# A hybrid layer of scan, attention and experts: gate, convolution and the end of attention in another order within a step

## The chip, the cores and the metric

The kernel runs on one core of a Trainium2 chip. Its engines each work through their own instructions: TensorE (PE, matmuls), VectorE (DVE), ScalarE (ACT), GpSimd (POOL) and SyncE (SP, which here only issues DMAs). The metric is the device time of one execution in microseconds; lower is better. Three executions of the kernel before took 10,580.3, 10,592.63 and 10,608.76 us: the median is 10,592.63.

## The reference, cut to what matters

The input x is 16 images of 128 channels by 64x64 pixels, so 16 sequences of T=4096 tokens with 128 channels. Layer 0 is a state-space layer on the group-normed input, with 256 inner channels and 16 states:

```python
xz = u @ W_in;  xs, z = split(xz)            # 128 -> 256 + 256
xc = silu(conv(xs, conv_w, 4 taps, causal) + conv_b)
dt, Bm, Cm = split(xc @ W_xproj)             # 8 + 16 + 16
delta = softplus(dt @ W_dt + b_dt);  A = -exp(A_log)
h_new = exp(delta * A) * h + (delta * xc) * B      # a scan over the 4096 tokens, for each state
y = sum over states of h * C  + xc * D
x = x + (y * silu(z)) @ W_out
```

Layer 1 is an attention with running softmax (8 heads, each with one fixed query, cumulative over the tokens) on layer-normed tokens, and then experts:

```python
k, v = silu(ln(t) @ W_kv)                    # 8 heads x 128 each
s = q . k;   m_A = cummax(s);   e = exp(s - m_A);   u_A = cumsum(e)
t = t + mean over heads of cumsum(e * v) / u_A
t = t + experts(ln(t))                       # each of 64 experts takes its best 8 tokens
```

All arithmetic is float32, apart from some bf16 pieces inside the kernel.

## The kernel before, in words

**Blocks and steps.** The work of layer 0 and of the attention is cut into NK = 128 blocks of L = 512 tokens, 8 blocks per image. One loop over k (L713) runs both, interleaved. In its step k the scan works on block k (`cur`); block k-1 (`prev`) has its y turned back, gated and projected out; block k+1 (`nxt`) is normed, convolved and projected to delta, B and C; and the attention works on block k-9 (`m`: keys, scores, weights, values), on k-10 (`mp_`: the second half of its tokens) and on k-8 (`mn`: layernorm). Steps 0 to 8 have no attention; the last ten have no scan. After the loop come the routing, the experts and the last sum, which the change does not touch.

**States.** Within a step, a loop over the 16 states n (L896) does for each: the product `bx` of delta·x and B (DVE, L355); then `beside(n)` (L737), a list of pieces of all the other work, written out by hand for each n; then decays (ACT exps, L679), the load of B and C for a later state (SP, tile `bct`, L344), the two scans of the state (DVE, L361) with `between(n)` (L725) between them, the product with C (POOL), a copy of the last column (POOL), for some states a DMA that adds two products, and the sums over states on PE into `y_ps` (L388).

**What sets the order.** Every instruction goes through a small class `InOrder` (L23), which keeps the program's order on its engine; for that reason all of them carry line L31 in the profile. No scheduler moves anything. An engine that waits holds up all that follows it in this order. So `beside` and `between` are the schedule.

**Buffers.** [...] One bank is for the scores and the attention's sums (`s_ps`, `ao_ps`), two are for y, two for `bx`. The other three are a pool (`ps`, L83, given out by `bank`, L224) that goes round in the order of requests: keys, values, `yb_ps` (y turned back), `w_ps` (log weights), `o_ps` (output projection), `xs_ps` (convolution), `rest_ps`, `dbl_ps`, `z_ps`, `dt_ps` and others. A request that gets a bank waits until the last reader of its earlier content is done.

**The pieces that the change moves.** `turn_y` (L410) transposes y into two banks at n=2, and `gate` (L417) multiplies each by silu(z) on DVE. `out_proj` (L427) does four matmuls with W_out and two with the identity, which add the residual. `conv(k, a, taps)` (L286) is a convolution half `a` of the 256 channels: two matmuls for each tap with its shifted input. `conv_silu` (L295) does both silus on ACT. `weights(m, c)` (L607) forms the log weights of the 128 tokens c by matmuls and takes their exps on ACT into `wm`; `attend` (L624) multiplies them with the values and forms the carried sums, `carry_on` (L645) copies these out, and `attend_before` (L649) adds what came before the 128 tokens. `add_x` (L655) adds the residual and `finish` (L660) scales the result on ACT and writes it out with a DMA that ACT issues. `score_max` (L521) and `score_less` (on DVE) take the running maximum of the scores, `score_exp` the exp (ACT), `score_sum` the running sum (DVE) and `score_log` (L554) its log (ACT). `rest`, `split` (L568, L577) cut the logs into three bf16 parts, which `store_parts` (L581) writes out as `pd` and `spread_parts` (L586) reads back in 16 small DMAs into the tiles `lh` and `rh`, the inputs of `weights`. `store_bc` (L318) writes B and C out as `bcs`, from where `load_bc` reads them back, copied to all partitions. `gn_end` (L242) finishes, in five parts, the group norm of the next image, in one step of eight.

Of the kernel before, what the change touches and what calls it, by code (L numbers as in the profile page):

```python
# [11 lines left out]
ALU = mybir.AluOpType  # L12
# [27 lines left out]
def conv_attn_hybrid(ctx: ExitStack, tc: tile.TileContext, x, w_in, conv_w, conv_b, w_xproj, w_dt, b_dt,  # L40
# [8 lines left out]
    NH2 = DI // P  # L49
# [31 lines left out]
    with ExitStack() as st:  # L81
# [136 lines left out]
        def load_exp():  # L218
            tc.keep_in_program_order(nc.scalar.preload_act_table_set(EXP_LN))  # L219
# [194 lines left out]
                for c in range(L // P):  # L414
                    PE.transpose(yb[:, bass.ts(c, P)], w["yt"][:, c, bass.ts(a, P)], ident)

        def gate(k):  # L417
            w = blocks[k]
            for a in range(NH2):
                DVE.tensor_tensor(w["z"][:, a, :], w[f"yb{a}"], w["z"][:, a, :], ALU.mult)  # L420

        def tokens_of(w):

# [3 lines left out]
        def out_proj(k):  # L427

            w = blocks[k]
            w["o"] = bank("o_ps")  # L430
            for a in range(NH2):
                PE.matmul(w["o"], wo[:, a, :], w["z"][:, a, :], start=(a == 0), stop=False)
            PE.matmul(w["o"].rearrange("p (j i) -> p j i", j=L // HH), ident, tokens_of(w), start=False, stop=True)
# [211 lines left out]
        def carry_on(m, c):  # L645

            ACT.copy(carry[:, c, :], att[m].pop(("cp", c))[:, :P])

        def attend_before(m, c):  # L649
            s = att[m]  # L650
            if m % NBLK or c:
                PE.matmul(s["o"][:, bass.ts(c % 2, P)], carry[:, (c - 1) % 4, :], s["e"][:, c, :], start=False,
                          stop=True, skip_group_check=True)
# [59 lines left out]
        for k in range(NK + LAG + 1):  # L713
            b, i = divmod(k, NBLK)
            cur = k if k < NK else None
            prev = k - 1 if 0 <= k - 1 < NK else None
# [20 lines left out]
            def beside(n):  # L737

                if n == 0:
                    if mp_ is not None:  # L740
                        attend_before(mp_, 1)
                        add_x(mp_, 0)
                    if m is not None:
                        key(m, 0), key(m, 1), key(m, 2)
                    if mp_ is not None:
                        finish(mp_, 0)
                    if prev is not None:
                        if N - 3 in PAIRS:
                            add_y(prev, N - 3)
                        else:  # L750
                            add_y(prev, N - 2)
                if n == 1:
                    if m is not None:
                        key(m, 3), key(m, 4)
                        score(m, 0)
                    if prev is not None:
                        if N - 3 in PAIRS:
                            add_y(prev, N - 2)
                        add_y(prev, N - 1)
                    if nxt is not None:  # L760
                        norm_block(nxt)
                    if cur is not None:
                        skip(cur)
                    if prev is not None:
                        take_y(prev)
                if n == 2:
                    if m is not None:
                        key(m, 5), key(m, 6), key(m, 7)
                    if prev is not None:
                        turn_y(prev)  # L770
                    if cur is not None:
                        add_y(cur, -1)
                if n == 3:
                    if m is not None:
                        score(m, 1)
                    if prev is not None:
                        gate(prev)
                    if mp_ is not None:
                        for x in range(4, 8):
                            value(mp_, x // 2, x % 2)  # L780
                if n == 4:
                    load_exp()
                    if m is not None:
                        score_max(m)
                    if mp_ is not None:
                        weights(mp_, 2)
                    if ends is not None:
                        gn_end(ends, 1)
                if n == 5:
                    if mp_ is not None:  # L790
                        attend(mp_, 2)
                        weights(mp_, 3)
                    if m is not None:
                        score_exp(m)
                    if prev is not None:
                        out_proj(prev)
                    decays(k, n, 2)
                    if mp_ is not None:
                        carry_on(mp_, 2)
                if n == 6:  # L800
                    if mp_ is not None:
                        attend(mp_, 3)
                        attend_before(mp_, 2)
                    if nxt is not None:
                        conv(nxt, 0)
                    decays(k, n, 2)
                    if prev is not None:
                        put_back(prev)
                    if mp_ is not None:
                        carry_on(mp_, 3)  # L810
                    if ends is not None:
                        gn_end(ends, 3)
                if n == 7:
                    if mp_ is not None:
                        attend_before(mp_, 3)
                        add_x(mp_, 1)
                    if m is not None:
                        score_log(m)
                    if mp_ is not None:
                        finish(mp_, 1)  # L820
                    if m is not None:
                        rest(m, 1)
                        split(m, 1)
                    if nxt is not None:
                        conv(nxt, 1, range(KC // 2))
                    decays(k, n, 2)
                    if m is not None:
                        rest(m, 2)
                        split(m, 2)
                        store_parts(m)  # L830
                        inverse(m)
                    if nxt is not None:
                        conv(nxt, 1, range(KC // 2, KC))
                    if nxt is not None:
                        conv_silu(nxt)
                    if ends is not None:
                        gn_end(ends, 4)
                if n == 8:
                    if cur is not None:
                        sums_of_y(n)  # L840
                    if m is not None:
                        turn_weights(m)
                        value(m, 0, 0)
                    if nxt is not None:
                        xproj(nxt)
                        store_bc(nxt)
                    if m is not None:
                        value(m, 0, 1)
                if n == 9:
                    if mn is not None:  # L850
                        ln_center(mn)
                        ln_square(mn)
                    if cur is not None:
                        gate_silu(cur)
                    if k + 2 < NK:
                        load_block(k + 2, ACT)
                    if m is not None:
                        value(m, 1, 0), value(m, 1, 1)
                if n == 10:
                    if mn is not None:  # L860
                        ln_var(mn)
                    if nxt is not None:
                        delta(nxt)
                    load_exp()
                    if mn is not None:
                        ln_scale(mn)
                if n == 12:
                    if m is not None:
                        weights(m, 0)
                if n == 13:  # L870
                    if m is not None:
                        attend(m, 0)
                        attend_before(m, 0)
                        weights(m, 1)
                    decays(k, n, 2)
                    if m is not None:
                        carry_on(m, 0)
                if n == 14:
                    if mn is not None:
                        ln_apply(mn)  # L880
                    if m is not None:
                        attend(m, 1)
                    decays(k, n, 2)
                    if m is not None:
                        carry_on(m, 1)
                if n == 15:
                    if stat is not None:
                        gn_stats(*stat)
# [7 lines left out]
            for n in range(N):  # L896
# [2 lines left out]
                if ends is not None and n == 2:  # L899
                    gn_end(ends, 0)  # L900
                beside(n)
                if n in (4, 11, 12, 15):
                    decays(k, n, 2)
                if cur is not None:
                    later = k * N + n + LEAD_BC
# [320 lines left out]
```

## Time and profile before

| | |
|---|---|
| median of three executions | 10,592.63 us (10,580.3 to 10,608.76) |
| the profiled execution | 10,585.55 us |
| its span (first to last instruction) | 10,583.8 us |
| PE, DVE busy | 9294.7 us (88%), 9048.4 us (85%) |
| ACT, POOL busy | 7298.5 us (69%), 7402.2 us (70%) |
| mean granted clock of TensorE | 0.933 |
| loop over k with scan and attention | about 640 to 9255 us |
| HBM | 143 GB/s over the span |

Times in the profile are in us from the span's start. In its lists of instructions, `out<-in` are the program's tile names, a number after x is a count, and a bracket tells how long the engine was idle just before and which instruction's end released it. PEld is the loading of weights, which runs beside the matmuls. The ends of matmuls are modelled, so a busy PE isn't always a PE at its peak rate.

### The profile page before, as it was taken

Reading aid. Unit: us, or ns where it says so; the run is one execution under the profiler, and the core shown is the slowest. Engines: PE = TensorE matmul, PEld = TensorE weight load, DVE = VectorE, ACT = ScalarE, POOL = GpSimd, SP = SyncE. Lnnn points to the kernel's source line nnn. Section 1 sums busy time; section 2 is a strip of 40 time slices with the busy share of each in tenths; the row PEclk is TensorE's granted clock in tenths of the full one; section 3 lists DMA queues with packets and bytes.
Section 4 is the critical chain, followed back from the end, with each engine's and each line's share of the span. In section 5 each row is a group of like instructions: output and inputs, shape, how many; then the busy total and the mean of one; then the engine's idle time right before and its main releaser. Section 6 shows DMA issues by size and latency. Waiting matters only on the chain.

```text
span 10583.8 us, 163130 instructions
## 1 busy us (share of the span) xinstructions
PE 9294.7 (88%) x58461; PEld 5670.1 (54%) x58461; DVE 9048.4 (85%) x9987; ACT 7298.5 (69%) x12924; POOL 7402.2 (70%) x4387
## 2 busy tenths in 40 slices
PE   5679999999999999999999999999999999988775
PEld 3345555555555555555555555555555555555652
DVE  8999999999999999999999999999999999921743
ACT  4567777777777777777777777777777777755740
POOL 7888787778787777878777878877787878810000
PEclk7789999999999999999999999999999999999886
DMA  6676666666666666666666766666666666611348
GB/s 172 172 188 171 179 169 180 165 179 173 162 183 161 183 166 181 173 177 170 170 177 168 185 166 186 170 178 170 176 167 173 178 165 181 161 50 39 110 157 355
DMA packets 889083, 1794.66 MB, mean 170 GB/s; under 512 B 96896, under 2 KB 182544, under 8 KB 881104
## 3 DMA queue, kind: packets, MB, share of 16 engines
q1 hardware_dynamic: 732912, 1414.88, 46.4%
q0 software_dynamic: 73728, 268.47, 12.8%
q10 hardware_dynamic: 81632, 100.88, 3.0%
q8 instruction: 463, 7.59, 0.3%
q14 instruction: 348, 2.85, 0.1%
HBM read 1363.98 MB, written 151.52 MB: 143 GB/s over the span
## 4 chain that ended last, share of the span: by engine, by line
PE 61%; ACT 25%; DVE 5%; issue 4%; DMA 3%; POOL 1%; ACTq 1%; SPq 0%; DVEq 0%; POOLq 0%
PE ao_ps L31 9%; PE v_ps L31 9%; PE k_ps L31 8%; ACT da L31 8%; PE y_ps L31 6%; PE carry_ps L31 4%; PE o_ps L31 4%; PE xs_ps L31 4%; ACT wm L31 3%; ACT L219 3%; PE s_ps L31 3%; PE dbl_ps L31 3%; PE dt_ps L31 2%; DVE h L31 2%; PE z_ps L31 2%
## 5 line engine op out<-in xcount | busy, mean ns | idle before, releaser
L31 POOL TENSOR_TENSOR da<-h,bct 128x1024 f32<-128x1024 f32 x2048 | 6600.5, 3223 | 1815.7 <-DVE h L31 812.8
L31 DVE TENSOR_TENSOR_SCAN h<-da,state,bx 128x512 f32<-128x512 f32 x3584 | 4415.2, 1266 | 169.7 <-DVE bx L31 1.9
L31 DVE TENSOR_TENSOR bx<-du,bct 128x1024 f32<-128x1024 f32 x2048 | 2653.7, 1296 | 160.4 <-DMA bct<-bcs 92.0
L31 ACT ACTIVATE da<-delta,a_neg 128x512 f32<-128x512 f32 x4096 | 2628.0, 716 | 42.6 <-DMA da<-da 42.4
L31 PE MATMUL y_ps<-ident,da 128*128 128x128 f32 x12288 | 1800.4, 302 | 237.5 <-DMA da<-da 129.6
L31 PEld LDWEIGHTS y_ps<-ident,da 128*128 128x128 f32 x12288 | 1575.8, 157 | 659.4 <-issue 375.1
L31 PE MATMUL v_ps<-wv,xn 128*128 128x512 f32 x2048 | 1053.8, 639 | 306.8 <-ACT xc L31 299.0
L31 PE MATMUL ao_ps<-wm,v 128*128 128x128 f32 x8192 | 1055.1, 283 | 180.5 <-ACT wm L31 180.5
L31 PEld LDWEIGHTS ao_ps<-wm,v 128*128 128x128 f32 x8192 | 994.1, 195 | 401.6 <-ACT wm L31 246.3
L31 ACT ACTIVATE v<-v_ps 128x512 f32<-128x512 f32 x1024 | 610.2, 597 | 758.3 <-PE v_ps L31 718.0
L31 PE MATMUL k_ps<-xn,wk 128*128 128x512 f32 x2048 | 942.6, 593 | 0.0
L31 PE MATMUL xs_ps<-xb,wc 128*128 128x512 f32 x2048 | 938.0, 594 | 1.8 <-issue 1.8
L31 PEld LDWEIGHTS v_ps<-wv,xn 128*128 128x128 f32 x2048 | 349.9, 195 | 832.7 <-ACT xc L31 326.7
L31 ACT ACTIVATE wm<-w_ps 128x512 f32<-128x512 f32 x1024 | 552.1, 591 | 340.2 <-PE w_ps L31 338.3
L31 ACT ACTIVATE kt<-k_ps 128x512 f32<-128x512 f32 x1024 | 599.5, 600 | 234.4 <-PE k_ps L31 211.5
L31 DVE TENSOR_TENSOR_SCAN h<-da,bx 128x512 f32<-128x512 f32 x512 | 599.9, 1206 | 25.5 <-ACT da L31 0.5
L31 PEld LDWEIGHTS xs_ps<-xb,wc 128*128 128x128 f32 x2048 | 361.6, 191 | 380.5 <-issue 366.0
L31 PEld LDWEIGHTS k_ps<-xn,wk 128*128 128x128 f32 x2048 | 370.2, 190 | 318.5 <-issue 282.9
L31 POOL COPY state<-h 128x2 f32<-128x2 f32 x1792 | 518.1, 289 | 0.0
L31 POOL DMA_DIRECT2D da<-da x512 | 449.1, 877 | 92.1 <-POOL state L31 35.7
L31 ACT ACT_TABLE_LOAD x395 | 506.8, 1283 | 7.7 <-issue 1.5
L31 ACT ACTIVATE xs<-ao_ps 128x256 f32<-128x256 f32 x256 | 97.5, 381 | 438.3 <-PE ao_ps L31 438.3
(196 smaller groups left out, 10679.1 us busy)
## 6 DMA issues: line engine op xcount, KB each, us to landing
bct<-bcs SPq DMA_DIRECT2D x2048, 512.0 KB
da<-da POOLq DMA_DIRECT2D x512, 512.0 KB, 7.9
xs<-t_d SPq DMA_DIRECT2D x240, 256.0 KB
xs<-in_x_dram SPq DMA_DIRECT2D x128, 256.0 KB
xt<-in_x_dram SPq DMA_DIRECT2D x64, 512.0 KB
t_d<-xt SPq DMA_DIRECT2D x64, 512.0 KB
t_d<-xs ACTq DMA_DIRECT2D x256, 128.0 KB
t<-t_d SPq DMA_DIRECT2D x128, 256.0 KB
```

Of the source, the lines that this page charges most:

```text
L31: return lambda *args, **kw: self.tc.keep_in_program_order(f(*args, **kw))
L219: tc.keep_in_program_order(nc.scalar.preload_act_table_set(EXP_LN))
```

## The change

Pieces of `beside` are moved; nothing is added to the computation or taken from it. `gate` now does one half per call.

- The gate of block k-1, both halves at n=3 before, is done half by half: half 0 at n=4 ahead of the running maximum, half 1 at n=5.
- The first half of the convolution of block k+1 moves from n=6 (behind the attentions 2 and 3) to n=4, behind the log weights 2 and ahead of attention 2.
- The log weights 3 and the output projection move from n=5 to n=6.
- The last three pieces of the attention of block k-10 (`attend_before` 3, `add_x`, `finish`) move from n=7, where they were ahead of `rest`, `split` and the second half of the convolution, to n=8, behind the convolution's silus; `attend_before` 2 moves from n=6 to the end of n=5.
- Log weights 0, attention 0 and its carry move one state earlier (n=12, 13 to n=11, 12), with the decays of n=12 behind the attention; log weights 1 stay at n=13.
- The last part of the group norm moves from the end of n=7 to the end of n=8.

```diff
-        def gate(k):
-            w = blocks[k]
-            for a in range(NH2):
-                DVE.tensor_tensor(w["z"][:, a, :], w[f"yb{a}"], w["z"][:, a, :], ALU.mult)
+        def gate(k, a):
+            w = blocks[k]
+            DVE.tensor_tensor(w["z"][:, a, :], w[f"yb{a}"], w["z"][:, a, :], ALU.mult)
...
                 if n == 3:
                     if m is not None:
                         score(m, 1)
-                    if prev is not None:
-                        gate(prev)
                     if mp_ is not None:
                         for x in range(4, 8):
                             value(mp_, x // 2, x % 2)
                 if n == 4:
                     load_exp()
+                    if prev is not None:
+                        gate(prev, 0)
                     if m is not None:
                         score_max(m)
                     if mp_ is not None:
                         weights(mp_, 2)
+                    if nxt is not None:
+                        conv(nxt, 0)
                     if ends is not None:
                         gn_end(ends, 1)
                 if n == 5:
+                    if prev is not None:
+                        gate(prev, 1)
                     if mp_ is not None:
                         attend(mp_, 2)
-                        weights(mp_, 3)
                     if m is not None:
                         score_exp(m)
-                    if prev is not None:
-                        out_proj(prev)
                     decays(k, n, 2)
                     if mp_ is not None:
                         carry_on(mp_, 2)
+                        attend_before(mp_, 2)
                 if n == 6:
                     if mp_ is not None:
+                        weights(mp_, 3)
+                    if prev is not None:
+                        out_proj(prev)
+                    if mp_ is not None:
                         attend(mp_, 3)
-                        attend_before(mp_, 2)
-                    if nxt is not None:
-                        conv(nxt, 0)
                     decays(k, n, 2)
...
                 if n == 7:
-                    if mp_ is not None:
-                        attend_before(mp_, 3)
-                        add_x(mp_, 1)
                     if m is not None:
                         score_log(m)
-                    if mp_ is not None:
-                        finish(mp_, 1)
-                    if m is not None:
                         rest(m, 1)
                         split(m, 1)
...
                         conv_silu(nxt)
-                    if ends is not None:
-                        gn_end(ends, 4)
                 if n == 8:
                     if cur is not None:
                         sums_of_y(n)
+                    if mp_ is not None:
+                        attend_before(mp_, 3)
+                        add_x(mp_, 1)
+                        finish(mp_, 1)
                     if m is not None:
                         turn_weights(m)
                         value(m, 0, 0)
...
                     if m is not None:
                         value(m, 0, 1)
+                    if ends is not None:
+                        gn_end(ends, 4)
...
+                if n == 11:
+                    if m is not None:
+                        weights(m, 0)
                 if n == 12:
-                    if m is not None:
-                        weights(m, 0)
-                if n == 13:
                     if m is not None:
                         attend(m, 0)
                         attend_before(m, 0)
+                    decays(k, n, 2)
+                    if m is not None:
+                        carry_on(m, 0)
+                if n == 13:
+                    if m is not None:
                         weights(m, 1)
                     decays(k, n, 2)
-                    if m is not None:
-                        carry_on(m, 0)
...
-                if n in (4, 11, 12, 15):
+                if n in (4, 11, 15):
                     decays(k, n, 2)
```

## The prediction

> **What bounds the kernel now.** I read the page first: busy shares, the 40 slices, and the chain of work that ended last.
>
> ```profile
> PE 9294.7 (88%) x58461; PEld 5670.1 (54%) x58461; DVE 9048.4 (85%) x9987; ACT 7298.5 (69%) x12924; POOL 7402.2 (70%) x4387
> PEclk7789999999999999999999999999999999999886
> PE 61%; ACT 25%; DVE 5%; issue 4%; DMA 3%; POOL 1%; ACTq 1%; SPq 0%; DVEq 0%; POOLq 0%
> ```
>
> PE and DVE are about equally busy, but the chain is PE and ACT. The steady part runs from 640 to 9255 us: some 118 steps of k at a mean of 73.0 us. Steps 0 to 8 (about 65 us each) lack the attention, those from k=128 (about 48 us) lack the convolution. So the change is worth what it does to one steady step, times 118.
>
> Next, the waits between 2000 and 8000 us, which is 82 steps (columns: total us, times, longest).
>
> ```profile
> PE v_ps L31 <- ACT xc L31: 209.4, 82, 2.6
> DVE z L31 <- PE yb_ps L31: 148.7, 82, 2.8
> PE ao_ps L31 <- ACT wm L31: 101.9, 163, 1.9
> PE o_ps L31 <- ACT wm L31: 60.7, 82, 0.7
> ACT v L31 <- DMA bct<-bcs: 28.0, 8, 4.6
> ```
>
> Per step PE loses 2.55 us waiting for the convolution's silus, 1.24 before the attentions and 0.74 before the output projection; with smaller ones, 5.9 of 73. The gate makes DVE wait 1.8 us per step, but the chain inside a step goes from PE to ACT and back and never through the gate. Third, the timeline of PE, DVE and ACT in one step without disturbance. I count its times from the end of the second score matmul, 4954.98; the step is 71.85 us long.
>
> ```profile
> 4952.69 1.29 DVE L31 TENSOR_TENSOR z<-yb_ps,z 128x512 f32<-128x512 f32 x2 [1.08 <-PE yb_ps L31]
> 4957.52 0.41 DVE L31 TENSOR_TENSOR_SCAN mx<-negc,s_ps 128x128 f32<-128x128 f32 x1
> 4961.20 2.09 PE L31 MATMUL ao_ps<-wm,v 128*128 128x128 f32 x16 [0.91 <-ACT wm L31]
> 4972.23 3.60 PE L31 MATMUL xs_ps<-xb,wc 128*128 128x512 f32 x8
> 4977.40 0.39 ACT L31 ACTIVATE xs<-ao_ps 128x256 f32<-128x256 f32 x1 [4.19 <-PE ao_ps L31]
> 4984.98 1.13 PE L31 MATMUL v_ps<-wv,xn 128*128 128x512 f32 x2 [2.55 <-ACT xc L31]
> 4986.04 1.91 PE L31 MATMUL dbl_ps<-xc,wx 128*40 128x512 f32 x4
> 4988.60 0.33 ACTq L31 DMA_DIRECT2D bcs<-dbl  x1
> ```
>
> The same x-projection one step later, in PE's timeline:
>
> ```profile
> 5058.02 3.21 PE L31 MATMUL dbl_ps<-xc,wx 128*40 128x512 f32 x4
> ```
>
> And both stretches in the windows view (length; busy us of PE, PEld, DVE, ACT, POOL; granted clock; DMA share; GB/s):
>
> ```profile
> 5055.00:5062.00 7.00, 5.04 (x7) 1.31 (x8) 6.70 (x6) 3.88 (x7) 6.44 (x3) 0.76 0.74 203
> 4983.00:4990.00 7.00, 5.02 (x11) 1.74 (x12) 6.70 (x6) 4.60 (x9) 6.41 (x3) 1.00 0.67 184
> ```
>
> After the 2.55 us wait the clock drops to half in about every second step, and four x-projection matmuls take 3.21 us instead of 1.91. Together with the values beside them such a step loses 1.65 us; over the steps, about 0.7.
>
> [...] stretches at 0.5 start on a grid of 3.41 us. [...] In the timeline no matmul overtakes another, so one that waits for a bank holds up all later ones. [...]
>
> **The change part by part**, per steady step.
>
> *Gate in two states.* Same two DVE instructions, 0.65 us each. At n=3 they waited 1.8 us; at n=4 and 5 PE has long turned y, so the wait goes. It was slack: 0 on the chain by itself. But gate 0 (0.65) and gate 1 now stand in other places. Score's maximum starts at 2.5 before and about 3.1 after; from there to the next product DVE takes 4.30 us (4957.52 to 4961.82), then product 5 1.14 and gate 1 0.69: gate 1 ends 6.13 us after the maximum starts. Meanwhile both turned halves hold their banks longer. In the built program the four values of n=3 get the remaining bank and that of gate 0, so weights 2 must wait for a silu of the last value: its end goes from 4.2 to 4.95. The first convolution half gets the bank of gate 1: **a new wait of PE for DVE**. Its matmuls could start at 5; gate 1 ends at 6.35 at the earliest. Cost 1.2 to 1.6 us. Queued behind it: y sums, attention 2, carry, weights 3, o, so everything.
>
> *Convolution half ahead of attention 2.* Eight matmuls, 3.44 us, moved. They cover the 0.91 us wait for wm (ACT ready at 6.2). Gain 0.91. The 0.74 before o remains, since o follows weights 3 by the same 1.47 us and takes over a bank that ACT's exps read.
>
> *End of attention behind the silus.* Two matmul groups (0.22 of earlier state, 0.43 of x) go from before rest to after the y sums, into the 2.55 us wait: PE's work is the same, the wait shrinks by 0.65 to 1.9. On ACT one scaling (0.39) and one DMA issue (0.33) move behind two splits, the issue of pd and the silus. ACT waited 4.19 us for that scaling; now it waits for rest instead, which is on time either way (0). The moved DMA to t_d is read only after the steady phase (0). But SP's and ACT's DMAs are dealt round over eight completion semaphores, each waiting for the previous DMA on its own. By program order bcs now follows the first of the 16 spread transfers lh<-pd, which is issued about 6.9 us after pd and lands some 1.4 later: 8.3, where ACT reaches bcs at 7.3. **ACT stalls about 1.0 us in every step**; queued behind are the value's silu, the square and the gate's silus, and PE waits for them through their banks. About 0.4 of it reaches PE. In return the old neighbour goes: in one step of eight bcs waited 4.6 us for a bct (the last line of the waits above), which cost PE 3.11 and the step about 2.9, or 0.36 on average.
>
> *Weights, attention, carry of m one state earlier, decays behind.* No instruction added. They cover waits of PE for wm (0.43 at 48.8) and carry (0.37). PE gains about 0.45 there at most; but then the key matmuls merely come earlier, and the loop below does not pass through them. 0.
>
> *gn_end 4* moves one state later, in one step of eight, off nothing: 0.
>
> **The sum.** PE alone: 0.75 (weights 2) + 1.35 (gate 1) − 0.91 − 0.65 + 0.4 (bcs) − 0.45 gives +0.5; but the first two waits make up for each other when DVE comes early. I prefer the loop that binds. DVE, from rstd to gate 1: xn and product 0 8.83, four states of 3.85 (15.4), product 4 1.14, gate 0 0.61, maximum stretch 4.30, product 5 1.14, gate 1 0.69: 32.1. PE and ACT from there back to rstd: convolution 3.44, y 0.87, attention 2 with carry and earlier state 3.24, weights 3 to o 1.47, o 3.52, attention 3 2.79, y 0.87, then rest to the value 7.8, value to rstd 15.8, bcs 0.4: 40.2. Together 72.3 for a clean step, 72.6 if bcs costs more than 0.4; I take 72.45 against 71.85: +0.6. Against that, the drops of the clock (0.7) become rare, since the idle time is 1.9 and not 2.55 with real matmuls ahead; I keep 0.25 of it, bounded by 0 and 0.9. And 0.36 of the eighth step goes. So 72.45 + 0.25 = 72.7 against 73.0: −0.3 × 118 = −35 us. The step before: 71.85 + 0.7 + 0.36 is 72.9, the measured 73.0 nearly. Head and tail steps: at most 0.5 us of 9 each, neglected.
>
> The profiled execution took 10,585.55 us (span 10,583.8), 7 below the median of 10,592.63. The change is applied to the median: **10,557 us**.
>
> **Rivals.** *Faster by 1 to 2%.* DVE doesn't bind: it reaches gate 1 before PE wants the bank, because without the wait at the gate (1.8) it runs ahead. For: DVE is 93% busy in the steady part, hence 5 us of slack in a step. Against: xn already waits for rstd in 45 of 82 steps, which ties DVE's start to PE. PE alone then gives 71.85 − 0.91 − 0.65 + 0.75 = 71.05, with 0.25 left of the cold clock: −1.7 × 118, some 10,390 to 10,420.
>
> *Slower.* Convolution behind gate 1: each us by which gate 1 is later than 6.35 holds PE's queue in full. The change breaks even where the clean step reaches 72.75 with 0.25 of cold clock, so where the wait is 0.3 us longer than in my loop. With 1 us more (or the new idle of PE at the convolution dropping the clock, 1.65 in half of the steps), the step is 73.7: +80 us, some 10,675.
>
> *No change.* The removed waits were slack of DVE and ACT (the chain, with 5% of DVE, speaks for it), and the PE waits removed come back at gate 1: 10,590.
>
> **How the numbers follow.** The loop above 0.5 (its own range 10,500 to 10,600, from 0 to 0.9 of cold clock and 0.3 either way on the loop), faster rival 0.2, slower 0.2, no change 0.1. A tenth is left out on either side, half of each outer rival: 10,420 to 10,665. A run of this kernel can tell about 0.3%, 32 us. Of the loop's 0.5, 0.28 lies beyond that, 0.16 within, 0.06 slower. Faster 0.48, same 0.26, slower 0.26.
>
> **What would show it.** Right: no wait of DVE for yb; a wait of xs_ps for DVE z of about 1.3 us in every step; v for xc at 1.9; no ACT wait of 4.19; ACT 1 us behind bcs for lh; fewer x-projections of 3.2 us. Wrong: a wait at xs_ps near 0 (the faster rival) or above 2.5 (the slower), a step time below 71.5 or above 73.3, or the clock lost at a new place.

## The result, and the profile after

The changed kernel took 10,510.32 us (median of three, 10,500.43 to 10,519.05), against 10,592.63 before: a ratio of 0.993, 95% interval 0.9914 to 0.9946, or 82 us. That is inside the stated range and on the side that was forecast, but the gain is more than twice the 36 us of the forecast.

The page of the kernel after: busy shares, granted clock by slices, chain of the work that ended last.

```profile
PE 9306.2 (89%) x58461; PEld 5584.4 (53%) x58461; DVE 8947.7 (85%) x9987; ACT 7317.3 (70%) x12924; POOL 7411.9 (71%) x4387
...
PEclk7789999999999999999999999999999999998886
...
PE 46%; DVE 23%; ACT 18%; issue 9%; DMA 4%; ACTq 1%; SPq 0%; POOL 0%; DVEq 0%; POOLq 0%
```

Busy times hardly differ. The chain does: DVE has gone from 5% to 23% of it. The waits between 2000 and 8000 us, now 83 steps (total us, times, longest), say where it enters:

```profile
PE v_ps L31 <- ACT xc L31: 137.5, 83, 1.7
...
DVE xn L31 <- ACT rstd L31: 107.1, 81, 3.0
...
PE xs_ps L31 <- DVE z L31: 98.8, 83, 1.4
...
PE o_ps L31 <- ACT wm L31: 62.0, 83, 1.0
...
ACT v L31 <- DMA lh<-pd: 8.1, 5, 2.1
...
PE ao_ps L31 <- ACT wm L31: 5.2, 10, 0.6
```

DVE no longer waits for yb. PE's wait for the silus is 1.66 us a step (2.55 before), the one ahead of the attentions is nearly gone (5.2 us in all against 101.9), and a new one stands in every step: the convolution for gate 1, 1.19 us. One clean step in the timelines of DVE, PE, SP and ACT (scores done at 4977.42):

```profile
4977.35 0.68 DVE L31 TENSOR_TENSOR z<-yb_ps,z 128x512 f32<-128x512 f32 x1
...
4983.06 0.68 DVE L31 TENSOR_TENSOR z<-yb_ps,z 128x512 f32<-128x512 f32 x1
...
4983.80 3.70 PE L31 MATMUL xs_ps<-xb,wc 128*128 128x512 f32 x8 [1.25 <-DVE z L31]
...
5007.74 1.12 PE L31 MATMUL v_ps<-wv,xn 128*128 128x512 f32 x2 [1.66 <-ACT xc L31]
5008.80 1.91 PE L31 MATMUL dbl_ps<-xc,wx 128*40 128x512 f32 x4
...
5008.89 0.26 SPq L31 DMA_DIRECT2D lh<-pd  x1
...
5011.35 0.33 ACTq L31 DMA_DIRECT2D bcs<-dbl  x1
```

The x-projection takes 1.91 us here, and in all 118 steps it takes under 2.3; before, 56 of 118 took 2.4 to 3.6. The rest of this document counts in such steps, from the end of one second score matmul to the next. A matmul is called cold here when it runs at half clock. In the traces of both kernels the granted clock is 1.00 or 0.50, nothing between: the windows view of the kernel before has 0.50 from 5058.48 to 5061.88, which takes in most of the prediction's x-projection of 3.21 us. Before, all 243 stretches at 0.50 start on multiples of 3.41 us, counted from the first, to within 0.02 us.

| 118 steps | before | after |
|---|---|---|
| mean, us | 73.00 | 72.31 |
| a clean step (the most frequent length without group norm and without a cold matmul), us | 71.85 | 71.5 |
| PE time lost to half clock, about, us per step (busy time above the median of all steps: x-projection, values, convolution, output projection, delta) | 0.97 | 0.56 |
| mean of the 14 steps with the group norm, us | 75.2 | 75.0 |

The sum of the steps fell by 81.0 us of the 85.1 us between the two spans. So half of the gain is the clean step (−0.35), and the other half is of the size of what the clock takes less (−0.4; a cold matmul can also fall into a wait, so the two need not add up to the 0.69 exactly).

### The profile page after: what moved, and what is told of

Same layout as the page of the kernel before. It is cut to its first block, busy times and chain, and to the rows that moved or that the text cites. A ratio compares the mean times of both kernels' runs of the same rounds, so it can differ in the third digit from the quotient of the medians.

```text
span 10498.7 us, 163128 instructions
## 1 busy us (share of the span) xinstructions
PE 9306.2 (89%) x58461; PEld 5584.4 (53%) x58461; DVE 8947.7 (85%) x9987; ACT 7317.3 (70%) x12924; POOL 7411.9 (71%) x4387
## 4 chain that ended last, share of the span: by engine, by line
PE 46%; DVE 23%; ACT 18%; issue 9%; DMA 4%; ACTq 1%; SPq 0%; POOL 0%; DVEq 0%; POOLq 0%
DVE h L31 11%; DVE bx L31 8%; ACT da L31 7%; PE ao_ps L31 6%; PE y_ps L31 6%; PE v_ps L31 5%; PE xs_ps L31 4%; PE o_ps L31 4%; PE carry_ps L31 3%; PE k_ps L31 3%; PE dt_ps L31 2%; PE dbl_ps L31 2%; PE z_ps L31 2%; PE w_ps L31 2%; ACT wm L31 2%
## 5 line engine op out<-in xcount | busy, mean ns | idle before, releaser
L31 DVE TENSOR_TENSOR bx<-du,bct 128x1024 f32<-128x1024 f32 x2048 | 2608.0, 1273 | 261.9 <-DMA bct<-bcs 195.0
L31 ACT ACTIVATE da<-delta,a_neg 128x512 f32<-128x512 f32 x4096 | 2603.0, 718 | 35.7 <-DMA da<-da 30.6
L31 PE MATMUL y_ps<-ident,da 128*128 128x128 f32 x12288 | 1773.8, 297 | 203.5 <-POOL da L31 103.8
L31 PEld LDWEIGHTS y_ps<-ident,da 128*128 128x128 f32 x12288 | 1534.0, 153 | 629.2 <-issue 372.6
L31 PE MATMUL v_ps<-wv,xn 128*128 128x512 f32 x2048 | 1031.5, 625 | 207.2 <-ACT xc L31 193.8
L31 PE MATMUL xs_ps<-xb,wc 128*128 128x512 f32 x2048 | 987.9, 620 | 141.3 <-DVE z L31 139.5
L31 PE MATMUL ao_ps<-wm,v 128*128 128x128 f32 x8192 | 1027.8, 279 | 54.7 <-ACT wm L31 45.3
L31 PEld LDWEIGHTS v_ps<-wv,xn 128*128 128x128 f32 x2048 | 317.0, 188 | 758.6 <-ACT v L31 251.1
L31 ACT COPY carry<-carry_ps 128x128 f32<-128x128 f32 x512 | 133.6, 261 | 539.3 <-PE carry_ps L31 539.3
```

The lines of the kernel that those rows point to most:

```text
L31: return lambda *args, **kw: self.tc.keep_in_program_order(f(*args, **kw))
```

## The experiments

Theory: the step is set by a loop from rstd through DVE (norm, products and scans, gate 0, maximum, product 5, gate 1) to the convolution, and from there through PE and ACT back to rstd. On top of that comes the clock. Rivals: DVE's wait at the gate was the cost; or the end of attention, or the weights of m, made the gain. Each ratio is to the kernel before, measured on the same chip in the same set; the kernel before had medians from 10,574 to 10,604 us in these sets, so between sets a difference of some 30 us is not read as one.

| run | median us | ratio (95%) | mean step | steps with a cold x-projection |
|---|---|---|---|---|
| the change | 10,510 | 0.9930 (0.9914 to 0.9946) | 72.31 | 0 |
| fin_back | 10,687 | 1.0084 (1.0064 to 1.0104) | 74.02 | 73 |
| m_back | 10,500 | 0.9912 (0.9894 to 0.9931) | 72.43 | 0 |
| gate_n3 | 10,371 | 0.9784 (0.9763 to 0.9805) | 71.26 | 0 |
| gates_n4 | 10,306 | 0.9727 (0.9710 to 0.9744) | 70.62 | 0 |
| conv_back | 10,477 | 0.9905 (0.9886 to 0.9924) | 71.98 | 2 |
| before_gates_n4 | 10,585 | 1.0006 (0.9994 to 1.0017) | 72.93 | 52 |
| before_warm | 10,490 | 0.9918 (0.9897 to 0.9939) | 72.22 | 0 |
| before_fin | 10,545 | 0.9972 (0.9962 to 0.9982) | 72.68 | 1 |
| before_fin_dma | 10,420 | 0.9854 (0.9832 to 0.9876) | 71.67 | 0 |
| gates_n4_dma | 10,340 | 0.9773 (0.9753 to 0.9792) | 70.93 | 0 |
| gates_n4_pair9 | 10,578 | 0.9997 (0.9988 to 1.0007) | 72.89 | 0 |
| gates_n4_gn | 10,295 | 0.9728 (0.9706 to 0.9750) | 70.39 | 0 |

### Is gate 1 in the loop?

Two other places for the gate, both on the changed kernel:

```diff
 gate_n3:   at n=3, behind score(m, 1)
+                        gate(prev, 0), gate(prev, 1)
 gates_n4:  at n=4, ahead of score_max(m)
-                        gate(prev, 0)
+                        gate(prev, 0), gate(prev, 1)
 both:      at n=5
-                        gate(prev, 1)
```

> The changed kernel with both gate halves back at n=3. Loop theory: gate 1 is done before PE wants its bank for the convolution, the 1.2 us wait of xs_ps for DVE goes, and the step is shorter by up to 1.2 us: about 10,370, with a wait of DVE for yb_ps of about 1.5 us again. Rival (the wait of DVE at the gate was what cost the time): most of the gain is lost, about 10,580.

> The changed kernel with gate 1 right behind gate 0 at n=4, ahead of the running maximum. Loop theory: gate 1 ends 1.3 us after the scores instead of 6.4, xs_ps waits no more, DVE doesn't wait for yb_ps either, the maximum starts 0.65 us later, which attention 2 doesn't see: step shorter by about 1.2 us, 10,370. Rival (gate 1 is not on the path): 10,510 within 0.3%.

Measured: 10,371 and 10,306. In both, PE's wait for gate 1 at xs_ps is gone. In gate_n3 DVE waits for yb again, and nothing of the gain is lost. That the time is just what the theory gave is in part luck: bcs now does wait for lh (first line below), PE waits 0.97 us a step at z_ps for that, and in return the steps with a group norm are shorter and no first convolution half is cold (19 in the change). gates_n4 gains more than the theory had (step 70.62): there the wait at z_ps is only 0.2 us, and again none of these convolutions is cold. The waits of gate_n3:

```profile
ACT v L31 <- DMA lh<-pd: 117.1, 42, 5.1
...
DVE z L31 <- PE yb_ps L31: 104.1, 78, 2.6
```

So the new wait was real and on the path, and it cost more than the change's own clean step gained. The same gate edit, made on the kernel before:

```diff
 before_gates_n4:  n=3 -> n=4, ahead of score_max(m)
-                        gate(prev)
+                        gate(prev)
```

> The kernel before with one edit: both gate halves at n=4, ahead of the running maximum. DVE no longer waits for yb_ps. Slack theory: DVE's 1.8 us were not on the chain, 10,593 within 0.3%, perhaps +20 for values that wait for the banks. Rival (DVE's wait cost time): up to -1.8 x 118, about 10,380.

Measured: 1.0006, no difference. DVE's 1.8 us at the gate vanish and come back as other waits of DVE, here for B and C and for rstd (148.2 and 123.2 us, against 61.1 and 54.8 before); PE's waits stay.

```profile
PE v_ps L31 <- ACT xc L31: 210.3, 82, 2.7
...
DVE bx L31 <- DMA bct<-bcs: 148.2, 71, 4.8
...
DVE xn L31 <- ACT rstd L31: 123.2, 70, 3.3
```

### The other parts, undone one by one

```diff
 fin_back:  n=8 -> n=7, ahead of score_log and rest
-                        attend_before(mp_, 3); add_x(mp_, 1); finish(mp_, 1)
+                        attend_before(mp_, 3); add_x(mp_, 1); finish(mp_, 1)
 m_back:    weights(m, 0) at n=12, attend(m, 0) and carry_on(m, 0) at n=13 again
 conv_back: n=4 -> n=6, behind attend(mp_, 3)
-                        conv(nxt, 0)
+                        conv(nxt, 0)
```

> The changed kernel with one part undone: earlier state, x and the scaling with its DMA are back at n=7, ahead of rest. Loop theory (rstd, DVE to gate 1, convolution, PE and ACT back to rstd): the 0.65 us of matmuls return into the loop, each step is 0.65 us longer, +77 us on the changed kernel's 10,510: about 10,587. PE's wait for the silus goes back from 1.66 to about 2.4, ACT's wait for the scaled sum returns, and pd, which is then queued behind the 128 KB write, lands about 2 us later. Rival (this end of attention was slack, since ACT only waits elsewhere): 10,510.

> The changed kernel with one part undone: log weights 0, attention 0 and carry of block m are one state later again (n=12, 13). Loop theory: the loop does not pass there, so 10,510 within 0.3%. Rival (the covered waits for wm and carry, 0.45 us a step, are part of the gain): +53 us, about 10,563.

> The changed kernel with the first half of the convolution back at n=6, behind attention 3. Loop theory: its wait for gate 1 (1.2 us) goes, the wait for wm ahead of attention 2 (0.9 us) returns: -0.3 x 118 = -35 us, about 10,475. Rival (the convolution as cover is what made the gain): +0.9 x 118, about 10,615.

m_back makes no difference that can be measured, as the theory had it, though PE waits for wm and carry again there (66.3 and 31.2 us over 83 steps). conv_back gave 10,477, at the theory's number, but not by its bookkeeping: the wait at xs_ps went, and what came back stood at the output projection, which now waits for a carry, and hardly ahead of the attentions.

```profile
PE o_ps L31 <- ACT carry L31: 130.7, 76, 1.8
...
PE ao_ps L31 <- ACT wm L31: 18.0, 83, 0.6
```

So as long as gate 1 stood ahead of it, the convolution's new place gained nothing; whether it cost the 33 us can't be told, since the two ratios' intervals overlap.

fin_back missed: +177 us (+163 by the ratios) and not +77. Its steps without a cold x-projection or convolution and without a group norm take 72.4 us in the median, 0.9 more than the change's 71.5 (the theory had 0.65). The rest is the clock. With the wait for the silus back at 2.56, the x-projection is cold in 73 of 118 steps, which is 0.85 us a step (timeline of one of them):

```profile
5037.69 1.12 PE L31 MATMUL v_ps<-wv,xn 128*128 128x512 f32 x2 [2.56 <-ACT xc L31]
5038.74 3.33 PE L31 MATMUL dbl_ps<-xc,wx 128*40 128x512 f32 x4
```

So the end of attention behind the silus carries the whole gain of the change: without it the other moves together make the kernel 0.8% slower than the kernel before. The expectation was also wrong on pd, which did not land later (lh follows it after 4.7 us, against 5.1 in the change); of that below.

### The clock by itself

```diff
 before_warm, in turn_weights:
             et = bank("et_ps")
+            for _ in range(4):
+                PE.matmul(et[:, P:].rearrange("p (h d) -> p h d", d=P), ident, wv[:, :3, :], start=True, stop=True)
             PE.transpose(et[:, :P], s.pop("w"), ident)
```

> The kernel before with four more matmuls of 128x384 float32, whose result nothing reads, into the unused columns of the bank of et_ps. They run in PE's 2.55 us wait for the silus and take about 1.3 us of it. Clock theory: with 1.3 us less of idle time no x-projection runs at half clock (56 of 118 steps before, 1.45 us apart in their mean), and the kernel gets faster though it has more work: about -0.7 x 118 = -80 us, 10,510. Rival (the idle time itself is the cost, or the clock drops for another reason): unchanged at 10,593, or slower if the matmuls push the values back.

Measured: 10,490, and no cold x-projection in 118 steps. The added matmuls took twice the time that I had put down, 2.6 us, and fill the wait for the silus entirely (timeline):

```profile
5003.80 2.75 PE L31 MATMUL et_ps<-wv,ident 128*128 128x384 f32 x8
...
5006.63 1.13 PE L31 MATMUL v_ps<-wv,xn 128*128 128x512 f32 x2
5007.68 1.91 PE L31 MATMUL dbl_ps<-xc,wx 128*40 128x512 f32 x4
```

The clean step stays at 71.85, so the whole gain, 0.78 us a step, is the clock (counted as in the table of steps, the loss falls from 0.97 to 0.10; the mean granted clock of the profiled execution is 0.956, against 0.933 before). The change removes the cold x-projections too, by shortening the wait to 1.66 us: before_fin below shortens it alone, to the same 1.66, and 1 of 118 is left; fin_back brings the 2.56 back, and 73 return. In the runs with a mean wait of 1.66 us at most 2 of 118 x-projections are cold; means of 2.55 to 2.57 go with 52 (before_gates_n4), 56 (before) and 73 (fin_back).

### The write of B and C, and what sets it free

```diff
 before_fin:      the kernel before with attend_before(mp_, 3), add_x, finish at n=8 alone
 before_fin_dma, gates_n4_dma:  finish only scales; its write comes at n=9
                     if k + 2 < NK:
                         load_block(k + 2, ACT)
+                    if mp_ is not None:
+                        write_half(mp_)
```

> The kernel before with one part of the change alone: attend_before 3, add_x and finish behind the silus, at n=8. Loop and clock theory: 0.65 us less per step (-77), the wait for the silus 1.9 us and no cold x-projections (-80), but bcs now waits for the first transfer of lh, since in this kernel the spread starts 6.9 us after pd (+0.4 x 118 = +47): about 10,480. Rival (this part is slack and the gate made the gain): 10,593.

> The kernel before with the end of attention behind the silus, as in the run of that part alone, but with the write of the scaled half issued later still, behind the load of xb at n=9. So bcs gets the semaphore of pd again and not that of the first lh transfer. Theory (the stall of ACT behind bcs, some 2 us in each step, swallowed what this part gives): PE's wait of 1.1 us at z_ps goes, the clean step falls from 71.9 to about 71.2, and the time to about 10,440. Rival (another loop holds the clean step at 71.85): 10,544, as without this edit.

before_fin missed its 10,480: it gave 10,545. Cold x-projections went (1 of 118 left), but the clean step didn't get shorter: ACT stalls behind bcs for lh by 1.8 us at the median, and PE waits at z_ps. The traces show the sharing that the prediction speaks of: eight semaphores serve all DMAs of SP and ACT (698 or 699 DMAs each, before and in the change), and the last DMA ahead of bcs on its semaphore is pd in 103 of 118 steps before and a load of lh in 103 here, a bct in 14 of both.

```profile
ACT v L31 <- DMA lh<-pd: 109.5, 46, 4.1
...
PE z_ps L31 <- ACT v L31: 88.5, 80, 3.8
```

With the write issued later, bcs shares pd's semaphore in 117 of 118 steps of before_fin_dma, PE's wait at z_ps nearly goes, and the time is 10,420:

```profile
PE z_ps L31 <- ACT v L31: 3.2, 8, 0.6
```

Part of that gain is the stall behind bct in one step of eight, which went as well. Thus the stall that the prediction put into the change (1.0 on ACT, 0.4 on PE) exists in before_fin, at 1.8 on ACT and 0.8 on PE in the seven other steps. In the change bcs shares with lh as predicted (117 of 118), but ACT waited for lh in only 5 of 83 steps. The reason is when the spread starts. The first lh follows pd after 6.97 us before (medians, here and below), 7.5 in before_fin and 6.7 in gates_n4, but after 5.1 in the change. What goes along with it is the 512 KB pair sum that POOL issues for state 7: 2.2 us ahead of pd before, 1.3 in before_fin, 2.1 in gates_n4, and 4.5 in the change. The gate edit alone does that: before_gates_n4 has 4.6, and lh after 5.5. From the pair sum to the first lh it is 8.8 to 10.1 us in all runs but gate_n3 (7.3) and the next one, which moves that sum in gates_n4:

```diff
 gates_n4_pair9
-        PAIRS = (1, 3, 5, 7)
+        PAIRS = (1, 3, 5, 9)
```

> The kernel with both gate halves at n=4, with POOL's fourth pair sum formed at state 9 instead of 7; states 6 and 7 are then added on PE singly, 8 and 9 as a pair, the same number of matmuls. In all traces the first lh is issued 9 to 10 us after the 512 KB pair sum of state 7. Theory (pd's transfer queues behind that sum): with no sum ahead of it, lh follows pd after about 3 us instead of 6.7, ACT's wait behind bcs goes, some 10,250 if the sum, now later, harms nothing. Rival (pd takes its time for another reason): 6.7 us as before and 10,306 or slower.

> The kernel with both gate halves at n=4 ahead of the maximum, and the same later issue of the write. In that kernel ACT waits 0.8 us a step for lh behind bcs, as the prediction said for the change itself. Theory: the wait goes, -0.4 to -0.8 us a step: about 10,240. Rival (ACT's wait is covered): 10,306.

lh followed pd after 3.1 us in the median, with single steps from 2 to over 7. One step of gates_n4 and one of gates_n4_pair9 (timelines):

```profile
5045.40 0.33 ACTq L31 DMA_DIRECT2D pd<-parts  x1
5051.88 0.26 SPq L31 DMA_DIRECT2D lh<-pd  x1
...
5115.05 0.33 ACTq L31 DMA_DIRECT2D pd<-parts  x1
5117.32 0.29 SPq L31 DMA_DIRECT2D lh<-pd  x1
```

So the sum ahead of pd is what makes pd late: with it elsewhere, 3.1 us in place of 6.7. How it does so was not shown. But it isn't the landing of the whole sum that is waited for: in gate_n3, where the sum is issued only 0.5 us ahead of pd, lh comes after 6.5 us, in the median 1.2 us before the sum has landed. The kernel of this run was no faster than the kernel before, 10,578: attention 0 now runs cold in every step (3.45 us in the step below, where attention 3 takes 1.96; mean granted clock 0.921, against 0.948 in gates_n4), behind two new waits of PE (timeline).

```profile
5059.35 0.58 PE L31 MATMUL w_ps<-rh,lh 64*128 64x512 bf16 x1 [1.42 <-ACT rstd L31]
...
5061.18 3.45 PE L31 MATMUL ao_ps<-wm,v 128*128 128x128 f32 x16 [0.68 <-ACT wm L31]
```

gates_n4_dma missed too: 10,340, slower than gates_n4 (the intervals of their ratios don't meet). ACT's wait for lh went, but DVE waited longer for B and C (104.1 us in place of 64.7), and in one step of eight bcs now waits for a write of x (35.7 us in 10 steps). So the gain that this edit had in before_fin_dma does not come again here; which of the two waits made it slower was not told apart.

### The eighth step

The prediction gave 0.36 us per step for bcs no longer waiting for bct in the steps with a group norm. That wait did go (1.4 us at z_ps before, averaged over these steps, 0 after), yet they take 75.0 us, hardly less than 75.2. The timelines of ACT and PE in one of them:

```profile
5634.15 5.40 PE L31 MATMUL xs_ps<-xb,wc 128*128 128x512 f32 x8 [1.38 <-DVE z L31]
...
5639.70 0.16 ACT L31 COPY gs<-gn_ps 128x1 f32<-128x1 f32 x1 [5.30 <-PE gn_ps L31]
...
5645.16 0.37 PE L31 MATMUL w_ps<-rh,lh 64*128 64x512 bf16 x1 [1.24 <-ACT carry L31]
```

gn_end 1 stands at n=4 as ever, but its small matmul is now behind the convolution on PE, and ACT's copy of it holds up decays and carry, for which PE waits at w_ps: 1.8 us in these steps, 0.5 in others. The first of these lines also shows where the clock is lost now: this convolution took 5.40 us and not 3.70 (windows view: length; busy us of PE, PEld, DVE, ACT, POOL; clock; DMA share; GB/s).

```profile
5636.00:5640.00 4.00, 4.00 (x12) 1.98 (x11) 0.10 (x1) 0.30 (x2) 0.00 (x0) 0.72 0.55 156
```

Of the 0.56 us a step still lost after, 0.27 are such convolutions (19 of 118 steps, 32 us in all), 0.12 output projections and 0.11 the delta matmuls. They come with the new waits just ahead, 0.37 us at the log weights and 1.2 for gate 1: in gate_n3 and gates_n4, where both are gone, none of these convolutions is cold. The last run puts the small matmul ahead in gates_n4:

```diff
 gates_n4_gn:  n=4 -> n=3, ahead of score(m, 1)
-                        gn_end(ends, 1)
+                        gn_end(ends, 1)
```

> The kernel with both gate halves at n=4, and the second part of the group norm (one matmul, a copy on ACT, in one step of eight) ahead of the scores at n=3 instead of behind the convolution at n=4. Theory: in that step ACT waits some 3.5 us for the small matmul behind the convolution, the carry is copied late, and PE waits 1.6 us at w_ps where other steps wait 0.15; that goes, -1.45 x 15 steps = -22 us: about 10,284. Rival (the eighth step is long for its other work): 10,306.

10,295 against 10,306: the time alone can't tell the two apart. The trace can: w_ps waits 0.1 us in these steps (1.6 in gates_n4), which now take 70.7 us and not 72.4. These two are the fastest versions of this study, 2.7% below the kernel before.

## Why the prediction was right or wrong

| us per step | predicted | measured |
|---|---|---|
| clean step | 72.45 | 71.5 |
| half clock | 0.25 | 0.56 |
| the rest, mostly the eighth step | 0 | 0.25 |
| sum | 72.7 | 72.3 |

- **The loop that binds: right in its parts, too long in the sum.** DVE from rstd to gate 1 measured 31.8 us (32.1 predicted), PE and ACT back to rstd 39.7 (40.2, of which 0.4 for bcs). I then took 72.45 where my terms gave 72.3, in case bcs cost more. So of the 0.95 that the clean step came out shorter, 0.4 is bcs, 0.15 that margin, and the rest small errors in many terms. gate_n3 and gates_n4 show that the loop through gate 1 did bind.
- **The new wait at xs_ps: right.** 1.19 us in each of 83 steps (1.2 to 1.6 predicted), gate 1 ending 6.4 us after the scores (6.35 at the earliest).
- **DVE's wait at the gate worth nothing: right**, 1.0006 in before_gates_n4.
- **Waits covered: right.** The 0.91 before attention 2 went, the 0.74 before o stayed, the silu wait fell to 1.66 (1.9 predicted). Log weights 2 do wait for a silu of the last value, 0.37 us. Weights 0 one state earlier: 0, as m_back shows.
- **bcs behind lh, 1.0 us in every step: wrong.** The step that failed took the 6.9 us from pd to lh from the kernel before. They depend on how far POOL's pair sum is ahead of pd. Without DVE's wait at the gate the sum comes earlier, and in the change it is 2.3 us further ahead than before. In gates_n4, where PE no longer waits for gate 1, pd comes 1.6 us earlier and the sum 0.9 us later than in the change; there the 6.7 is back, and bcs stands 0.9 us behind the end of dbl's copy, as predicted for the change, with 0.2 of it on PE.
- **The eighth step, −0.36: wrong.** The old wait went, but "off nothing: 0" looked at gn_end 4, which moved, and not at gn_end 1, which stayed while the convolution moved ahead of it.
- **The clock: right in kind, mis-sized.** The cold x-projections went altogether, 0.78 us a step by before_warm. But the new idle time ahead of the convolution made part of it cold, which I had left to the slower rival. 0.56 remained where I kept 0.25.

Two errors in opposite directions, a loop 0.95 too long and disturbances 0.55 too small, left the forecast 0.4 us a step, 47 us, too slow. That it came this close is luck: the loop's error alone would have made it 112 us too slow. The faster rival's mechanism (DVE reaches gate 1 before PE wants it) did not hold in the change, but gates_n4 makes it hold, and then its 10,390 to 10,420 are more than reached.

Open is why the wait of 2.55 us before went with a cold x-projection in 56 steps of 118 and not in the others. That the matmuls ahead of a wait count in this ("real matmuls ahead") was the author's estimate; it was not tried. Nor was it tried why attention 0 turned cold with the pair sum at state 9.

## What to carry to other kernels

When a matmul is moved to an earlier place, ask first who frees its output bank: here one gate instruction that stood 5 us too late held back some 200 of the 290 us that the new order could give (10,510 against 10,306). Removing an engine's wait that is slack may gain nothing (1.0006 here) and still change what others wait for, through what that engine then starts earlier (here a large DMA). And of each piece that stays in its place, ask what has been put ahead of it in the queue.

## What the runs showed of the hardware

More work can be faster: four unused matmuls, 2.6 us of PE time in each step, filled PE's wait of 2.55 us and made the kernel 0.8% faster; the steps with a cold x-projection went from 56 of 118 to none. And the first load that waits for a 192 KB store was issued 6.7 us after that store (gates_n4) when a 512 KB accumulating transfer of another queue was issued 2.1 us ahead of the store, 5.1 us when that was 4.5 us ahead (the change), and 3.1 us with none there (gates_n4_pair9; all medians).
